# A decoder layer on one core: small operations on VectorE in the last ten steps, chunks of every sixteenth token, and a fixed order for the last chunk's projections

## The chip, the core and the metric

The kernel runs on one core of a Trainium2 chip. Five engines work side by side, each through a queue of its own in order: TensorE (PE in the profile; PEld is its weight load) multiplies matrices into PSUM, VectorE (DVE) and ScalarE (ACT) read PSUM and SBUF, GpSimd (POOL) works on SBUF alone here, and SyncE (SP) issues the DMAs. The metric is the device time of one execution in microseconds; the times of before are 2703.99, 2704.08 and 2704.45, median 2704.08.

## The reference

One pre-norm decoder layer over x of shape (2, 2048, 512) in float32, with three residual blocks. LN is a layer norm without scale and shift.

```
x = x + Wo . attention(rope(Wq . LN(x)), rope(Wk . LN(x)), Wv . LN(x))   # 16 heads of 32
x = x + gelu(LN(x) @ ctx.T) @ ctx                                        # 77 context rows
x = x + clip((LN(x) @ sign(W).T) * scale + bias, -100, 100)
```

The attention has no mask: each of the 2048 queries of a batch row looks at all 2048 keys. The rotary embedding turns each pair of features by an angle that depends on the token's place. All of the rest treats tokens alike.

## The kernel before

A *batch* is one of the two rows of x. Its 2048 tokens are cut into 16 *chunks* of 128 tokens, one token to a partition; four chunks make a *block* of 512. Chunk `ch` holds tokens `ch * 128` to `ch * 128 + 127`.

**Projections** (`project_batch`, L175). For each chunk: `norm` (L150 to L164) takes the mean and variance on VectorE (`chunk_stats`), makes scale and shift by four small operations (`scale_and_shift`, L141 to L146; the power by -0.5 in L143 always on GpSimd, from the constant tile `minus_half`), and applies them on ScalarE (L157). `turn` transposes the result on TensorE. `times` multiplies by `wk`, `wq` and `wv`; `rotate` applies the rotary tables `cos` and `sin` on VectorE and adds the halves on GpSimd (L212); `transpose_qk` turns q and k through TensorE into the tiles that attention reads (q copied by ScalarE, k by VectorE). The transposes of a chunk come one chunk late (`held`). In the loop TensorE is kept filled by `lead` (block maxima for the first attention steps) and by pieces of the output work of earlier blocks (`background_between`). The last chunk stands behind the loop, from L247: its projections, the transposes of two chunks, the values of the last two chunks, the last two sets of maxima, and the split and the transposition of the maxima of attention's first unit (`split_maxima`, `turn_maxima`).

Here the order is the tile scheduler's, which sorts the instructions by its own model of their times, with source order as priority.

**Attention** (`Attention.run`). A batch has 32 *units* (a block's 256 queries of four heads), each of eight *steps* over two chunks of keys at a time. A step has two halves of two heads each. In a half TensorE forms scores (L552, onto a start given by the maxima, L537), and in the same place the block maxima for the unit ten steps ahead (L459, reduced on VectorE, L471; `AHEAD = STEPS + 2` is 10). ScalarE takes the exponential (L690), GpSimd adds the two chunks' weights (`sm`, L692). A step later TensorE multiplies the weights by the values (L570), and another step later adds up the sums (`total`, L584). So in a batch's last ten steps there are no maxima and no reductions. In this part the order on TensorE, VectorE, ScalarE and GpSimd is the source's, by `tc.manual_schedule`; SyncE's is the scheduler's. The tiles `dkk`, `dkq` and `dkv` (differences between key blocks) lie in the buffers of `wk`, `wq` and `wv`, so the next batch's weights can be loaded only when these have been read for the last time.

**Output work** (`after_attention`). A generator for each finished part of a block: output projection, residual, norm, context attention, norm, feed-forward (L343 to L364), store. Its pieces are taken by `background`, one at a time, between the halves of attention's steps. Elementwise work that doesn't read PSUM goes where `side()` says:

```
    alone = []

    def side():
        return nc.vector if alone else nc.gpsimd
```

`alone` is set only behind the last batch's attention. Of batch 0's last block, the first two chunks are in the queue during the last ten steps; the other two are worked off in batch 1's projections. All parts of the last block of batch 1 go to the list `tail` and are worked off at the end, with `side()` on VectorE.

**Loads.** `load_x` brings a chunk to SBUF through SyncE, two chunks ahead; `cos` and `sin` are loaded once, each partition's 16 chunks in pieces of 64 bytes.

Of the kernel before, what the change touches and what calls it, by code (L numbers as in the profile page):

```python
# [9 lines left out]
F32 = mybir.dt.float32  # L10
F32R = mybir.dt.float32r
BF16 = mybir.dt.bfloat16
AF = mybir.ActivationFunctionType
# [3 lines left out]
P = 128  # L17
B, S, D = 2, 2048, 512
H, DK = 16, 32
C = 77  # L20
ND = D // P
BLK = 512
NB = S // BLK
CPB = BLK // P
NCH = S // P
HQ = 256
NU = NB * ND * 2
STEPS = NCH // 2
AHEAD = STEPS + 2
# [7 lines left out]
def decoder_layer(  # L37
# [16 lines left out]
    nc = tc.nc  # L54
# [11 lines left out]
    ps_acc = ctx.enter_context(tc.tile_pool(name="ps_acc", bufs=1, space=bass.MemoryType.PSUM))  # L66


    def load_x(b, ch, pool=xpool):
        t = pool.tile([P, D], F32, tag="x", name=f"x_{b}_{ch}")  # L70
        nc.sync.dma_start(t, x[b, ch * P : (ch + 1) * P, :])
        return t

    def load_w(src, name):
# [9 lines left out]
    qkv = load_qkv()  # L84
    cos = const.tile([P, NCH, DK // 2], F32, tag="cos", name="cos")
    sin = const.tile([P, NCH, DK // 2], F32, tag="sin", name="sin")
    nc.sync.dma_start(cos, rope_cos.rearrange("(c p) d -> p c d", p=P))
    nc.sync.dma_start(sin, rope_sin.rearrange("(c p) d -> p c d", p=P))

    ident = const.tile([P, P], F32, tag="ident", name="ident")  # L90
    make_identity(nc, ident)
# [4 lines left out]
    ones = const.tile([P, DK], F32, tag="ones", name="ones")  # L96
    nc.vector.memset(ones, 1.0)
    minus_half = const.tile([P, CPB], F32, tag="minus_half", name="minus_half")
    nc.vector.memset(minus_half, -0.5)


    mts = []
# [37 lines left out]
    def scale_and_shift(engine, stats):  # L140
        y, off = stats[:, :, 2], stats[:, :, 3]  # L141
        engine.tensor_scalar(y, stats[:, :, 1], EPS, None, ALU.add)
        nc.gpsimd.tensor_tensor(y, y, minus_half[:, : stats.shape[1]], ALU.pow)  # L143
        engine.tensor_mul(off, stats[:, :, 0], y)
        engine.tensor_scalar(off, off, -1.0, None, ALU.mult)
        return y, off  # L146

    def chunk_norm(ahead, b, ch):  # L150
        xc = ahead.pop(0)
        stats = stats_tile(1)
        chunk_stats(xc, stats[:, 0, 0:2])
        y, off = scale_and_shift(nc.gpsimd, stats)
        yield
        xn = work.tile([P, D], F32, tag="w", name="xn")
        nc.scalar.activation(xn, xc, AF.Identity, bias=off, scale=y)  # L157
        if ch + 2 < NCH:
            ahead.append(load_x(b, ch + 2))
        yield xn  # L160

    def norm(ahead, b, ch):
        *_, xn = chunk_norm(ahead, b, ch)
        return xn  # L164

    def turn(xn):
        pt = ps_t.tile([P, ND, P], F32, tag="t", name="pt")
        for i in range(ND):
            nc.tensor.transpose(pt[:, i, :], xn[:, i * P : (i + 1) * P], ident)  # L169
        xnt = work.tile([P, ND, P], F32, tag="w", name="xnt")  # L170
        nc.scalar.copy(xnt, pt)  # L171
        return xnt
# [3 lines left out]
    def project_batch(b, ahead, att, xnt, wk, wq, wv):  # L176
        def times(dst, xnt, w, part=range(ND)):
            for i in part:
                nc.tensor.matmul(dst, xnt[:, i, :], w[:, i, :], start=(i == 0), stop=(i == ND - 1))  # L179

        def transpose_qk(ch, qk, which=(0, 1)):
            blk, c = divmod(ch, CPB)
            cols = slice(c * P, (c + 1) * P)
            for a in which:
                pt = ps_s.tile([P, ND, P], F32, tag="s", name="ptqk")
                for i in range(ND):
                    nc.tensor.transpose(pt[:, i, :], qk[:, a, i * P : (i + 1) * P], ident)  # L187
                (nc.vector.tensor_copy if a else nc.scalar.copy)((att.q, att.k)[a][blk][:, :, cols], pt)
            if c == CPB - 1 and 1 in which:
                att.open_block(blk)  # L190

        def values(ch, xnt, pool=None):
            pv = (pool or ps_s).tile([P, D], F32, tag="t" if pool else "s", name="pv")
            times(pv, xnt, wv)
            v = kvq.tile([P, D], F32, tag=f"v{ch}", name=f"v_{b}_{ch}")
            nc.scalar.copy(v, pv)
            att.v.append(v)


        def rotate(ch, a, ps, r):  # L200
            half = [P, H, DK // 2]
            cs = cos[:, ch, None, :, None].to_broadcast(half + [2])
            sn = sin[:, ch, None, :].to_broadcast(half)
            pairs = ps.rearrange("p (h i t) -> p h i t", i=DK // 2, t=2)
            t1 = r[:, 0, a, :].rearrange("p (h i t) -> p h i t", i=DK // 2, t=2)
            t2 = r[:, 1, a, :].rearrange("p (h i t) -> p h i t", i=DK // 2, t=2)
            nc.vector.tensor_tensor(t1, pairs, cs, ALU.mult)
            nc.vector.scalar_tensor_tensor(
                t2[:, :, :, 0], pairs[:, :, :, 1], -1.0, sn, ALU.mult, ALU.mult
            )  # L210
            nc.vector.tensor_tensor(t2[:, :, :, 1], pairs[:, :, :, 0], sn, ALU.mult)  # L211
            nc.gpsimd.tensor_add(r[:, 0, a], r[:, 0, a], r[:, 1, a])  # L212

        held = None
        for ch in range(NCH):
            if ch == (NB - 1) * CPB:
                drain()
            blk, c = divmod(ch, CPB)
            if c == 0:
                att.q.append(kvq.tile([P, ND, BLK], F32, tag=f"q{blk}", name=f"q_{b}_{blk}"))  # L220
                att.k.append(kvq.tile([P, ND, BLK], F32, tag=f"k{blk}", name=f"k_{b}_{blk}"))
            r = big.tile([P, 2, 2, D], F32, tag="s", name="r")
            xn = norm(ahead, b, ch + 1) if ch + 1 < NCH else None
            pk = ps_t.tile([P, D], F32, tag="t", name="pk")
            pq = ps_t.tile([P, D], F32, tag="t", name="pq")
            if ch == NCH - 1:
                break
            times(pk, xnt, wk)
            rotate(ch, 1, pk, r)
            att.lead(1)  # L230
            background_between(2)
            times(pq, xnt, wq)
            rotate(ch, 0, pq, r)
            background_between(2)
            if held is not None:
                transpose_qk(*held)
            held = (ch, r[:, 0])
            xnt_next = turn(xn)
            if ch < NCH - 2:
                values(ch, xnt)  # L240
            else:
                left = xnt
            background_between(2)
            xnt = xnt_next


        times(pk, xnt, wk)  # L247
        rotate(ch, 1, pk, r)
        transpose_qk(*held)
        values(ch - 1, left, ps_t)  # L250
        transpose_qk(ch, r[:, 0], (1,))
        for i in range(ND):
            times(pq, xnt, wq, (i,))
            if i % 2 == 0:
                att.lead(1)
        rotate(ch, 0, pq, r)
        att.lead(AHEAD)
        values(ch, xnt, ps_t)
        transpose_qk(ch, r[:, 0], (0,))
        att.split_maxima(0)  # L260
        att.turn_maxima(0)
        att.key_steps()

    alone = []

    def side():
        return nc.vector if alone else nc.gpsimd


    attending = []
# [25 lines left out]
    def after_attention(b, blk, ot, first, end):  # L298
# [41 lines left out]
        def feed_forward(c, pt):  # L340
            parts = [work_tile([P, D], name, F32R) for name in ("high", "low")]
            parts = [part.rearrange("p (i t) -> p i t", t=P) for part in parts]
            nc.scalar.copy(parts[0], pt)  # L343
            nc.vector.tensor_sub(parts[1], pt, parts[0])
            yield True
            pf = bank([P, D], "pf")
            for k, part in enumerate(parts):
                for i in range(ND):
                    nc.tensor.matmul(  # L349
                        pf,  # L350
                        part[:, i, :],
                        wf[:, i, :],
                        start=(k == 0 and i == 0),
                        stop=(k == 1 and i == ND - 1),
                    )
            y = work_tile([P, D], "y")
            nc.vector.tensor_mul(y, pf, fs)
            yield False
            side().tensor_add(y, y, fb)
            yield False  # L360
            side().tensor_scalar(y, y, -MAX_VAL, MAX_VAL, ALU.max, ALU.min)
            side().tensor_add(xs[c], xs[c], y)
            r0 = blk * BLK + (first + c) * P
            nc.sync.dma_start(out[b, r0 : r0 + P, :], xs[c])  # L364
            yield False

        def project_out(ps, cols):
# [64 lines left out]
    class Attention:  # L432
# [201 lines left out]
        def run(self):  # L634
# [36 lines left out]
            more = self.b + 1 < B  # L671
            for t in range(NU * STEPS):
                u, i = divmod(t, STEPS)
                if more and t == (NU - 1) * STEPS:
                    self.x_next = [load_x(self.b + 1, 0), load_x(self.b + 1, 1)]
                if more and t == NU * STEPS - STEPS // 2:
# [38 lines left out]
            while ends:  # L715
                finish()
            attending.clear()
            ordered.__exit__(None, None, None)
            return xnt

    xnt = turn(norm(x_next, 0, 0))
    for b in range(B):
        att = Attention(b)
        project_batch(b, x_next, att, xnt, *qkv)
# [59 lines left out]
```

## Time and profile before

| | before |
|---|---|
| times of three runs | 2703.99, 2704.08, 2704.45 us |
| profiled execution | 2704.63 us, span 2702.9 us |
| mean granted clock of TensorE | 0.996 |
| busy: PE, DVE, ACT, POOL | 2675.5, 1702.1, 1321.0, 1741.2 us |
| batch 0: first projection, end of attention | 10.2, about 1339 us |
| batch 1: end of attention, last matmul ends | about 2655, 2696 us |

How to read it: the span runs from the first instruction to the last, and 1.7 us of the execution lie around it. Busy time is the union of an engine's instructions. In a list of waits a line has the waiting instruction, what released it, the microseconds in total, how often and the longest one. A line of the timeline has start, duration, engine, line of the kernel, operation, output and inputs, shapes, and in brackets the idle time of the engine ahead of it with what ended it. The granted clock is the share of full clock that TensorE had.

### The profile page before, as it was taken

The page shows a single profiled execution, that of the slowest core. Times are in us where ns is not written, and L with a number is a line of the kernel's source. Part 1 is how long each engine was busy: PE and PEld are TensorE (multiplying, and loading weights), DVE is VectorE, ACT ScalarE, POOL GpSimd, SP SyncE. Part 2 cuts the span into 40 slices and gives each one's busy share as a digit, 9 for nine tenths or more (in the row PEclk, how much of TensorE's full clock was granted, in tenths as well). Part 3 has the DMA queues.
Part 4 walks back from the last instruction along what each step waited for, and adds up shares of the span by engine and source line. Part 5 has one row for each costly group of instructions (what it writes and reads, how often), then busy time and mean ns, then how long its engine had stood idle before and what let it go on. Part 6 is the DMA issues. An engine that isn't in the chain of part 4 may idle for free.

```text
span 2702.9 us, 70221 instructions
## 1 busy us (share of the span) xinstructions
PE 2675.5 (99%) x30756; PEld 1490.6 (55%) x30756; DVE 1702.1 (63%) x2852; ACT 1321.0 (49%) x2393; POOL 1741.2 (64%) x1888
## 2 busy tenths in 40 slices
PE   8999999999999999999999999999999999999998
PEld 4445555555555555555554455555555555555555
DVE  3446777666666766676244467766767667766754
ACT  2114555455546554555422155555555455546553
POOL 3227777567857785677634287766687567857772
PEclk9999999999999999999999999999999999999999
DMA  4010000000000000000201000000000000000000
GB/s 125 24 32 2 5 4 4 4 4 18 20 3 4 11 28 4 4 12 26 72 25 36 8 4 4 4 4 4 4 27 12 4 4 19 19 4 4 19 19 17
DMA packets 41859, 43.54 MB, mean 16 GB/s; under 512 B 24758, under 2 KB 24758, under 8 KB 41552
## 3 DMA queue, kind: packets, MB, share of 16 engines
q1 hardware_dynamic: 41552, 39.05, 4.9%
q8 instruction: 241, 3.95, 0.6%
q14 instruction: 66, 0.54, 0.1%
HBM read 26.58 MB, written 8.39 MB: 13 GB/s over the span
## 4 chain that ended last, share of the span: by engine, by line
PE 96%; POOL 2%; DVE 1%; DMA 1%; issue 0%; ACT 0%; SPq 0%; POOLq 0%; ACTq 0%
PE st L552 22%; PE acc L570 22%; PE ps L459 18%; PE acc L584 8%; PE po L369 4%; PE pq L179 4%; PE pk L179 4%; PE pv L179 4%; PE st L537 3%; PE pf L349 2%; PE pt L331 1%; PE po L395 1%; PE ptqk L187 1%; PE ph L376 1%; POOL sm L692 1%; PE pt L169 1%
## 5 line engine op out<-in xcount | busy, mean ns | idle before, releaser
L692 POOL TENSOR_TENSOR sm<-pw 128x512 f32<-128x512 f32 x1024 | 1295.1, 1272 | 597.3 <-ACT pw L690 594.4
L471 DVE TENSOR_REDUCE mx<-ps 128x1 f32<-128x512 f32 x2048 | 1308.7, 682 | 515.6 <-PE ps L459 513.1
L690 ACT ACTIVATE pw<-st 128x512 f32<-128x512 f32 x2048 | 1111.4, 595 | 952.5 <-PE ps L459 618.4
L459 PE MATMUL ps<-k,q 32*128 32x512 f32 x4096 | 1188.3, 639 | 0.8 <-DVE mx L471 0.8
L570 PE MATMUL acc<-pw,v 128*32 128x256 f32 x8192 | 656.6, 392 | 0.0
L584 PE MATMUL acc<-sm,ones 128*32 128x128 f32 x7680 | 390.4, 280 | 2.1 <-POOL sm L692 2.1
L570 PEld LDWEIGHTS acc<-pw,v 128*32 128x32 f32 x8192 | 162.2, 108 | 398.1 <-issue 379.7
L459 PEld LDWEIGHTS ps<-k,q 32*128 32x128 f32 x4096 | 352.3, 183 | 21.5 <-issue 12.9
L584 PEld LDWEIGHTS acc<-sm,ones 128*32 128x32 f32 x7680 | 248.6, 110 | 157.3 <-POOL sm L692 2.6
L552 PE MATMUL st<-q,dkv 32*128 32x256 f32 x2048 | 291.8, 402 | 0.0
L552 PE MATMUL st<-q,dkk 32*128 32x256 f32 x2048 | 291.1, 400 | 0.0
L552 PE MATMUL st<-q,dkq 32*128 32x256 f32 x2048 | 289.9, 400 | 0.0
L552 PE MATMUL st<-q,k 32*128 32x256 f32 x2048 | 262.8, 374 | 0.0
L552 PEld LDWEIGHTS st<-q,dkk 32*128 32x128 f32 x2048 | 175.4, 184 | 89.8 <-issue 51.4
L552 PEld LDWEIGHTS st<-q,dkq 32*128 32x128 f32 x2048 | 172.7, 184 | 80.1 <-issue 54.2
L552 PEld LDWEIGHTS st<-q,dkv 32*128 32x128 f32 x2048 | 175.7, 185 | 59.5 <-issue 26.6
L552 PEld LDWEIGHTS st<-q,k 32*128 32x128 f32 x2048 | 195.0, 187 | 14.1
L212 POOL TENSOR_TENSOR r<-r 128x512 f32<-128x512 f32 x64 | 81.1, 1268 | 147.4 <-DVE r L211 147.0
L604 DVE RECIPROCAL num<-num 128x128 f32<-128x128 f32 x128 | 120.3, 942 | 63.1 <-ACT num L598 63.1
L133 DVE BATCH_NORM_STATS2 st<-x 128x6 f32<-128x512 f32 x96 | 65.4, 686 | 94.7 <-DMA x<-in_x_dram 94.4
L179 PE MATMUL pk<-wk,xnt 128*128 128x512 f32 x256 | 117.2, 601 | 2.3 <-ACT xnt L171 1.4
L179 PE MATMUL pq<-wq,xnt 128*128 128x512 f32 x256 | 118.0, 602 | 0.0
(106 smaller groups left out, 1788.2 us busy)
## 6 DMA issues: line engine op xcount, KB each, us to landing
x<-in_x_dram SPq DMA_DIRECT2D x64, 256.0 KB, 2.7
out_dram<-x SPq DMA_DIRECT2D x32, 256.0 KB, 2.0
wk<-in_wk_t_dram SPq DMA_DIRECT2D x2, 1024.0 KB, 8.4
wq<-in_wq_t_dram SPq DMA_DIRECT2D x2, 1024.0 KB, 10.7
wv<-in_wv_t_dram SPq DMA_DIRECT2D x2, 1024.0 KB, 6.1
wo<-in_wo_t_dram SPq DMA_DIRECT2D x1, 1024.0 KB, 6.3
wf<-in_wf_t_dram SPq DMA_DIRECT2D x1, 1024.0 KB, 5.1
mrow<-mt SPq DMA_TRANSPOSE x62, 2.3
```

The costliest lines, as they stand in the source:

```text
L179: nc.tensor.matmul(dst, xnt[:, i, :], w[:, i, :], start=(i == 0), stop=(i == ND - 1))
L212: nc.gpsimd.tensor_add(r[:, 0, a], r[:, 0, a], r[:, 1, a])
L369: nc.tensor.matmul(ps, ot[:, i, cols], wo[:, i, :], start=(i == 0), stop=(i == ND - 1))
L459: nc.tensor.matmul(ps, self.q[qb][self.rows[h], g, q0 : q0 + P], self.k[kb][self.rows[h], g, :], start=True, stop=True,)
L471: nc.vector.tensor_reduce(mx[:, qc, h, kb : kb + 1], ps, AX.X, ALU.max)
L537: nc.tensor.matmul(self.st[h], ones_b[r, :], mrow[r, None, :].to_broadcast([DK, 2, HQ]), start=True, stop=False, skip_group_check=True,)
L552: nc.tensor.matmul(self.st[h][:, c, :], keys[r, g, kc * P : (kc + 1) * P], self.q[qb][r, g, hf * HQ : (hf + 1) * HQ], start=False, stop=Tr ...
L570: nc.tensor.matmul(acc[self.rows[h], 0, :], self.v[self.chunk(i, c)][:, d0 : d0 + DK], pw[:, h, c, :], start=(i == 0 and c == 0), stop=(i ...
L584: nc.tensor.matmul(acc[self.rows[h], 1, part], ones, sm[:, h, part], start=False, stop=(i == STEPS - 1), skip_group_check=True,)
L604: nc.vector.reciprocal(num[:, 1, part], num[:, 1, part])
L690: nc.scalar.activation(pw[:, h], self.st[h], AF.Exp, scale=SCALE)
L692: nc.gpsimd.tensor_add(sm[:, hs, :], pw[:, hs, 0, :], pw[:, hs, 1, :])
```

## The change

It has five parts, all in one edit.

1. **Tokens.** Chunk `ch` holds every sixteenth token: partition p has token `16 p + ch`. `load_x` and the store use the new view `tokens`; `cos` and `sin` are laid out to match, so that a partition's 16 chunks are one run of 1 KB.
2. **Function table.** `minus_half` is written by a ScalarE activation (Identity, scale -0.5 on `ones`) and not by a VectorE memset, so the first activation, with the load of its function table, comes ahead of the first norm.
3. **First norm.** The small operations of the very first chunk's norm go to VectorE; the power stays on GpSimd.
4. **Last chunk.** The projections of the last chunk of each batch are put in source order on TensorE and VectorE. The order is new: the last chunk's queries are projected ahead of the values of the chunk before, the query rotation comes ahead of the maxima, and the two sets of maxima stand behind the first and the last quarter of those values. `values` is split, so that the copy (`keep_values`) stands by itself.
5. **Last ten steps.** From step `NU * STEPS - AHEAD` of a batch on, `free` is set, and `side()` gives VectorE to the output work's pieces until that batch's attention ends.

```diff
+    def tokens(rows, ch):
+        return rows.rearrange("(p c) d -> c p d", c=NCH)[ch]
...
-        nc.sync.dma_start(t, x[b, ch * P : (ch + 1) * P, :])
+        nc.sync.dma_start(t, tokens(x[b], ch))
...
-    nc.sync.dma_start(cos, rope_cos.rearrange("(c p) d -> p c d", p=P))
-    nc.sync.dma_start(sin, rope_sin.rearrange("(c p) d -> p c d", p=P))
+    nc.sync.dma_start(cos, rope_cos.rearrange("(p c) d -> p c d", p=P))
+    nc.sync.dma_start(sin, rope_sin.rearrange("(p c) d -> p c d", p=P))
...
-    nc.vector.memset(minus_half, -0.5)
+    nc.scalar.activation(minus_half, ones[:, :CPB], AF.Identity, scale=-0.5)
...
-    def chunk_norm(ahead, b, ch):
+    def chunk_norm(ahead, b, ch, engine=nc.gpsimd):
...
-        y, off = scale_and_shift(nc.gpsimd, stats)
+        y, off = scale_and_shift(engine, stats)
...
-    def norm(ahead, b, ch):
-        *_, xn = chunk_norm(ahead, b, ch)
+    def norm(ahead, b, ch, engine=nc.gpsimd):
+        *_, xn = chunk_norm(ahead, b, ch, engine)
...
             times(pv, xnt, wv)
+            keep_values(ch, pv)
+
+        def keep_values(ch, pv):
             v = kvq.tile([P, D], F32, tag=f"v{ch}", name=f"v_{b}_{ch}")
             nc.scalar.copy(v, pv)
             att.v.append(v)
...
+        ordered = tc.manual_schedule(
+            engines={mybir.EngineType.PE, mybir.EngineType.DVE}
+        )
+        ordered.__enter__()
         times(pk, xnt, wk)
         rotate(ch, 1, pk, r)
         transpose_qk(*held)
-        values(ch - 1, left, ps_t)
+        times(pq, xnt, wq)
         transpose_qk(ch, r[:, 0], (1,))
-        for i in range(ND):
-            times(pq, xnt, wq, (i,))
-            if i % 2 == 0:
-                att.lead(1)
         rotate(ch, 0, pq, r)
+        pv = ps_t.tile([P, D], F32, tag="t", name="pv")
+        times(pv, left, wv, (0,))
+        att.lead(1)
+        times(pv, left, wv, range(1, ND))
+        keep_values(ch - 1, pv)
         att.lead(AHEAD)
         values(ch, xnt, ps_t)
         transpose_qk(ch, r[:, 0], (0,))
         att.split_maxima(0)
         att.turn_maxima(0)
+        ordered.__exit__(None, None, None)
         att.key_steps()
...
     alone = []
+    free = []
 
     def side():
-        return nc.vector if alone else nc.gpsimd
+        return nc.vector if alone or free else nc.gpsimd
...
-            r0 = blk * BLK + (first + c) * P
-            nc.sync.dma_start(out[b, r0 : r0 + P, :], xs[c])
+            nc.sync.dma_start(tokens(out[b], blk * CPB + first + c), xs[c])
...
                 u, i = divmod(t, STEPS)
+                if t == NU * STEPS - AHEAD:
+                    free.append(True)
...
             attending.clear()
+            free.clear()
...
-    xnt = turn(norm(x_next, 0, 0))
+    xnt = turn(norm(x_next, 0, 0, nc.vector))
```

## The prediction

> **What bounds the kernel now.** The page first: TensorE is busy all through, so only its idle time and its clock can give anything.
>
> ```profile
> span 2702.9 us, 70221 instructions
> PE 2675.5 (99%) x30756; PEld 1490.6 (55%) x30756; DVE 1702.1 (63%) x2852; ACT 1321.0 (49%) x2393; POOL 1741.2 (64%) x1888
> ```
>
> Next the waits of TensorE: what it stood for, and the total. Together they are 20.7 us, and the tail behind its last matmul is 6.6 us more.
>
> ```profile
> PE pt L169 <- ACT xn L157: 8.1, 1, 8.1
> PE acc L584 <- POOL sm L692: 2.1, 1, 2.1
> PE pk L179 <- DMA wk<-in_wk_t_dram: 1.0, 1, 1.0
> PE ptqk L187 <- POOL r L212: 0.8, 1, 0.8
> PE ps L459 <- DVE mx L471: 0.8, 1, 0.8
> ```
>
> Then the timeline of TensorE around the 2.1 us wait, near the end of batch 0. Eight score matmuls (L552) take 1.13 us before it and 2.08 us behind it.
>
> ```profile
> 1320.10 1.13 PE L552 MATMUL st<-q,dkk 32*128 32x256 f32 x8
> 1325.99 0.41 PE L584 MATMUL acc<-sm,ones 128*32 128x128 f32 x4 [2.14 <-POOL sm L692]
> 1331.86 2.08 PE L552 MATMUL st<-q,dkv 32*128 32x256 f32 x8
> ```
>
> The windows view has busy time of PE, PEld, DVE, ACT and POOL (instructions in brackets), then the granted clock, DMA share and GB/s. The clock is halved in two stretches, each behind a wait: one behind the 0.76 us wait for `mx` in batch 0's last chunk, one behind the 2.14 us wait.
>
> ```profile
> 205.00:208.30 3.30, 2.54 (x10) 1.16 (x10) 3.28 (x6) 0.00 (x0) 0.00 (x0) 1.00 0.00 0
> 208.30:211.70 3.40, 3.40 (x5) 1.37 (x5) 3.05 (x7) 0.00 (x0) 1.64 (x3) 0.50 0.00 0
> 1320.10:1323.80 3.70, 3.70 (x48) 2.17 (x44) 0.00 (x0) 2.87 (x6) 3.62 (x4) 1.00 0.02 4
> 1328.00:1338.10 10.10, 10.10 (x88) 5.33 (x82) 0.00 (x0) 3.34 (x7) 5.37 (x5) 0.50 0.95 331
> ```
>
> The timeline of GpSimd says why `sm` was late: the feed-forward's L361 and L362 stand ahead of it in the queue, and five sums then run without a pause.
>
> ```profile
> 1320.19 1.27 POOL L692 TENSOR_TENSOR sm<-pw 128x512 f32<-128x512 f32 x1
> 1321.42 1.95 POOL L361 TENSOR_SCALAR y<-y 128x512 f32<-128x512 f32 x1
> 1323.45 1.26 POOL L362 TENSOR_TENSOR x<-x,y 128x512 f32<-128x512 f32 x1
> 1324.68 6.16 POOL L692 TENSOR_TENSOR sm<-pw 128x512 f32<-128x512 f32 x5
> ```
>
> Last, TensorE in the last chunk of batch 0 (first two lines) and batch 1. In batch 0 both maxima came together, and the second took 2.32 us where one takes 1.14, since banks came free one by one.
>
> ```profile
> 203.87 1.14 PE L459 MATMUL ps<-k,q 32*128 32x512 f32 x8
> 205.77 2.32 PE L459 MATMUL ps<-k,q 32*128 32x512 f32 x8 [0.76 <-DVE mx L471]
> 1548.03 1.21 PE L459 MATMUL ps<-k,q 32*128 32x512 f32 x8
> 1554.57 0.66 PE L187 MATMUL ptqk<-ident,r 128*128 128x128 f32 x4 [0.84 <-POOL r L212]
> ```
>
> **Last ten steps on VectorE.** They begin in batch 0 where the block maxima end, at 1286.6 us. From there GpSimd runs two each of L359 (1.28), L361 (1.93) and L362 (1.28), 9.0 us, and L142, L144 and L145 once for two chunks (0.66). These go to VectorE; the power (L143, 0.73) stays. There, by the rows of the kernel's end, an addition takes 0.69 and the clamp 0.42, so 2 x (0.69 + 0.42 + 0.69) = 3.6 us, and 3 x 0.15 for the small ones. VectorE was busy 7.8 of those 50 us. GpSimd keeps a 1.27 us sum per half step of 1.85 us; the late sum comes at least 4.5 us sooner (the second chunk's three operations) and was 2.1 us late. So the wait goes: 2.14 us. The half clock behind it lasted 10.24 us by the granted clock (1327.9 to 1338.1); at full rate that work takes half, so 5.12 us. Sum 7.26. Bounds: 2.14, if the clock drops anyway, to 7.26; I take the upper, as the clock is full all the way from 211.7 to the wait.
>
> The added wait is VectorE's, for the power, which stands behind a sum (1290.75 to 1292.02): it lasts from about 1288.5 to 1292.9. The next entry in VectorE's queue is L344, not due until 1297.3, so it holds nobody; ScalarE's `xn` at 1294.26 finds its operands some 0.5 us earlier than now. In batch 1 the same steps hold no such work (its last blocks go to the tail list, and GpSimd runs only sums and two L607 there): 0.
>
> What is late next at this place: weights. The SyncE queue issued batch 1's `wk` at 1327.13 behind the second store (1324.75, landed 1326.73) and an `x` load at 1326.75. The store now leaves at about 1317, so `wk` waits for the last read of `dkk`, which shares its buffer, at 1321.2. A 1 MB load alone took 6.1 us there (`wv`, 1334.00 to 1340.09), the slowest at the start 10.7. `wk` lands at 1327.3 to 1331.9; the first `pk` matmul is due at 1339.07 - 7.26 = 1331.8. `wq` (free at 1325.4, due 1335.3) and `wv` (1329.1, due 1342.6) have more room. I take 0, bound 0.1.
>
> **Last chunk in source order.** The same matmuls, transposes and copies, on two engines in a fixed order: `pk`, 8 transposes, `pq`, 4 transposes, a quarter of `pv`, maxima, the rest of `pv`, maxima, `pv` of the last chunk, 4 transposes, `ptm`. VectorE turns `q` before the eight reductions, no longer behind them, so GpSimd's addition of `r` is done some 5 us before its transposes: the 0.84 wait goes. The two maxima stand 3 quarters (2.6 us) apart, and four reductions (2.48 us) fit between, so banks are free: batch 0's 0.76, its long 2.32 and its half-clock stretch (3.41 us, worth 1.7) go. I size these by the two batches: from the first `pk` matmul to the first `st` matmul is 192.91 to 215.21 = 22.30 us in batch 0, 1535.72 to 1555.71 = 19.99 in batch 1. Without the 0.84, batch 1 needs 19.15. One new wait: the second maxima end at +14.2, four reductions 2.5, `neg` 0.2, five small GpSimd operations (0.26 to start, 1.4 to run) reach +18.4, where `ptm` could start at +18.1: 0.3 us. So 2.85 in batch 0 and 0.54 in batch 1, sum 3.39. The 0.38 wait for `mrow` stays. Batch 0 alone also has the sign conversions of `wf` (1.98 and 1.22 us, now at 198.59 and 202.00), which may fall between the reductions: 2.0 us lost there and 1.7 of half clock at worst, nothing at best; I take nothing, since VectorE has idle stretches of 2.7 and 1.2 us there. The part's ends are then -0.3 and +4.0.
>
> **The start.** The first norm on VectorE: at the kernel's end the chain from L142 to ScalarE takes 1.29 us (2660.44 to 2661.73), at the start 2.73 (4.53 to 7.26), so `xnt` is ready 1.4 us earlier, at about 8.4. But `wk` landed at 10.08 and the `pk` matmuls began at 10.22. Gain 0.1. The first table load (1.28 us) moves from 3.58 to about 1.1; it ended at 4.86 with its activation at 7.26, so 0; `minus_half` is then ready at about 2.6, before the power at 4.6. `cos` and `sin` become rows of 1 KB. Now they block SyncE (11.12 us of issue for `sin`) and with it the third `x` load until 15.27, yet TensorE has no wait from 10.22 to 192.2, so 0, whatever loads now pass them. Bounds: a late `wk` costs its lateness; at most 1.4 is to be had if `wk` landed with `xnt`, plus a clock that rises one 3.41 us window sooner (1.7).
>
> **Every sixteenth token.** An `x` load or store stays 128 rows of 2 KB, now 32 KB apart in memory. No row has this pitch. The nearest is the weight load: a partition's four 2 KB rows lie 256 KB apart, and 1 MB took 6.1 us, no slower per byte than `x` (256 KB in 2.7). The far one is `cos` in 64 B pieces, 12.9 us. I take 0. Only the first two loads and the last store are on the path; other loads run two chunks (23 us) ahead.
>
> **Sum.** 7.26 + 3.39 + 0.1 = 10.75. The profiled execution took 2704.63 (span 2702.9 and 1.7 around it), 0.55 over the median 2704.08; it gives 2693.9, and against the median 2693.3.
>
> **Rivals.**
> - *The clock does not follow the wait* (0.06). Half clock has another cause and stays; gains are 2.14 + 3.39 - 1.7 + 0.1 = 3.9: 2700.1. For it: waits of 0.68 and 0.84 elsewhere were followed by no drop. Against: the only half-clock stretches between 13.8 and 2683 us begin 2.5 and 1.9 us behind these two waits. The Trainium skill (TensorE: Matmul & The Clock Gate, What's actually happening) has the clock halve after a whole idle window of about 3.4 us, which neither wait is; by that rule this rival would hold, and the granted clock here speaks against it.
> - *The last chunk gives nothing* (0.14): the conversions fall between reductions, or GpSimd takes `dkv` (1.27 us) ahead of the split. Only 7.36: 2696.7.
> - *GpSimd stays late* (0.04): 3.5 remain, 2700.6.
> - *The wait moves to the weights* (0.07): an `x` load that waits for ScalarE's second norm (about 1333) gets ahead of `wk`; it lands at 1339.4, 7.6 us late, with 5.1 of half clock: 2693.3 + 12.7 = 2706.0, no measurable change.
> - *Slower: the pitch* (0.05). The `x` rows 32 KB apart crawl, and the first `wk` stands behind two such loads. It decides from 10.75 + 5.4 = 16.2 us, 8.1 per load: 256 KB in 10.9 us and not 2.8, and gives 2710. For it only the 12.9 us of `cos`, whose pieces are 64 B. The Trainium skill (DMA: Bandwidth & Descriptors, Latency and other measured facts) finds copies at half rate with rows 4 MiB apart and 207 GB/s at 512 KiB; it has no 32 KiB, and no run here shows such pitches. Half rate would cost this start about 2 us.
> - *`wk` comes early too* (0.04): 2690 to 2691.5.
>
> **How the numbers follow.** My forecast has 0.60, its own range 2691 to 2696. 0.2%, about what can be told from no change here, is 5.4 us: 2698.7 and 2709.5. Faster: 0.60 + 0.14 + 0.04 = 0.78; within: 0.06 + 0.04 + 0.07 = 0.17; slower 0.05. The range 2690.0 to 2700.5 holds the forecast, the last-chunk rival, the early `wk` and the unmoved clock, 0.84.
>
> **What would show it.** Right: no wait of `acc` for `sm`; granted clock 1.00 from 13.8 us to the tail; 19.4 us from `pk` to `st` in both batches; at most 0.3 before `ptm`; first `pk` near 10.1; `x` loads landing in 2.7. Wrong: half clock at either place without a wait ahead, a wait of batch 1's `pk` for `wk`, L114 or L116 among the last chunk's reductions, or `x` loads that take several us more.

## The result and the profile after

The changed kernel took 2692.95 us (median of six runs, 2692.05 to 2693.68) against 2704.23 for the kernel before beside it: a ratio of 0.9961, 95% interval 0.9951 to 0.9971. The forecast was 2693.3, faster. The profiled execution took 2693.15 us, its span 2691.0.

The page and then the waits of TensorE in the changed kernel (waiting instruction, what released it, us in total, times, longest):

```profile
span 2691.0 us, 70222 instructions
PE 2668.3 (99%) x30756; PEld 1490.3 (55%) x30756; DVE 1710.0 (64%) x2863; ACT 1321.0 (49%) x2394; POOL 1732.8 (64%) x1876
```

```profile
PE pt L173 <- ACT xn L161: 7.4, 1, 7.4
PE pt L345 <- ACT sparek L339: 4.9, 3, 4.1
PE pk L183 <- ACT xnt L175: 1.3, 2, 0.7
PE pk L183 <- DMA wk<-in_wk_t_dram: 1.0, 1, 1.0
PE st L550 <- DVE mrow L511: 0.8, 2, 0.4
```

The three waits that the change was to touch are gone from the list: `acc` for `sm` (2.1), `ptqk` for `r` (0.8) and `ps` for `mx` (0.8). Note the busy time of TensorE: 2668.3 and not 2675.5, with the same 30,756 matmuls. Seven of the twelve microseconds were never idle time. They were the same matmuls at half clock, and the windows view shows where they went (busy time of PE, PEld, DVE, ACT and POOL with instructions in brackets, then the granted clock, DMA share, GB/s):

```profile
205.00:208.30 3.30, 3.30 (x13) 1.27 (x12) 3.05 (x5) 0.58 (x1) 0.00 (x0) 1.00 0.00 0
208.30:211.70 3.40, 3.40 (x12) 1.64 (x10) 1.90 (x4) 0.17 (x1) 1.11 (x6) 1.00 0.00 0
1319.06:1322.80 3.74, 3.74 (x54) 2.25 (x50) 0.00 (x0) 2.91 (x6) 3.74 (x4) 1.00 0.71 261
1322.80:1328.90 6.10, 6.10 (x96) 3.70 (x92) 0.00 (x0) 3.12 (x6) 3.95 (x4) 1.00 0.89 292
```

The two places that had 0.50 have 1.00. Cut at the first matmul of each stage, the two profiled executions differ so:

| stretch | before | after | gained |
|---|---|---|---|
| start to the first `pk` | 10.22 | 9.55 | 0.67 |
| first `pk` to the last chunk's `pk`, batch 0 | 182.70 | 183.65 | -0.95 |
| last chunk, `pk` to `st`, batch 0 | 22.30 | 19.22 | 3.08 |
| `st` to batch 1's first `pk` | 1123.86 | 1116.49 | 7.37 |
| to the last chunk's `pk`, batch 1 | 196.65 | 196.78 | -0.13 |
| last chunk, batch 1 | 20.00 | 19.18 | 0.82 |
| attention of batch 1 | 1099.31 | 1098.78 | 0.53 |
| from the tail's first `po` to the end | 47.82 | 47.34 | 0.48 |

They sum to 11.87, the difference of the spans but for rounding.

In the last chunk of batch 0, TensorE now runs without a pause from `pk` to `ptm` (timeline: start, duration, instruction, shapes, count):

```profile
193.20 3.70 PE L183 MATMUL pk<-wk,xnt 128*128 128x512 f32 x8 [0.68 <-ACT xnt L175]
...
202.52 1.14 PE L472 MATMUL ps<-k,q 32*128 32x512 f32 x8
203.60 2.84 PE L183 MATMUL pv<-wv,xnt 128*128 128x512 f32 x6
206.37 1.49 PE L472 MATMUL ps<-k,q 32*128 32x512 f32 x8
...
212.42 0.39 PE L550 MATMUL st<-mrow,ones_b 32*128 32x512 bf16 x2 [0.38 <-DVE mrow L511]
```

The two maxima stand 3.85 us apart; the second takes 1.49 us where it took 2.32. On VectorE the query rotation (`r`) had stood behind the eight reductions. First the timeline of the kernel before, then that of the changed kernel, where it stands ahead of them:

```profile
205.02 4.88 DVE L471 TENSOR_REDUCE mx<-ps 128x1 f32<-128x512 f32 x8 [1.80 <-PE ps L459]
210.04 0.68 DVE L207 TENSOR_TENSOR r<-pq,cos 128x512 f32<-128x512 f32 x1
```

```profile
202.29 0.68 DVE L214 TENSOR_TENSOR r<-pq,cos 128x512 f32<-128x512 f32 x1
...
203.65 1.29 DVE L484 TENSOR_REDUCE mx<-ps 128x1 f32<-128x512 f32 x2
204.86 1.22 DVE L120 TENSOR_SCALAR signs<-wf 128x2048 fp32r<-128x2048 f32 x1
205.99 1.28 DVE L484 TENSOR_REDUCE mx<-ps 128x1 f32<-128x512 f32 x2
```

In the last ten steps, the five sums that GpSimd runs without a pause (its timeline):

```profile
1316.72 6.20 POOL L707 TENSOR_TENSOR sm<-pw 128x512 f32<-128x512 f32 x5
```

The second of them, counted from the batch's end, is the one that had come late. It runs from 1317.94 to 1319.22 and is done 1.5 us ahead of its reader (1320.69); before, it was done 2.1 us behind the time at which its reader was due.

### The profile page after: what moved, and what is told of

The parts are those of the page before. It is cut to its first block, busy times and chain, and to the rows that moved or that the text cites. A ratio compares the mean times of both kernels' runs of the same rounds, so it can differ in the third digit from the quotient of the medians.

```text
span 2691.0 us, 70222 instructions
## 1 busy us (share of the span) xinstructions
PE 2668.3 (99%) x30756; PEld 1490.3 (55%) x30756; DVE 1710.0 (64%) x2863; ACT 1321.0 (49%) x2394; POOL 1732.8 (64%) x1876
## 4 chain that ended last, share of the span: by engine, by line
PE 98%; DVE 1%; DMA 0%; issue 0%; ACT 0%; POOL 0%; SPq 0%; POOLq 0%; ACTq 0%
PE st L565 23%; PE acc L583 22%; PE ps L472 18%; PE acc L597 8%; PE po L382 4%; PE pk L183 4%; PE pq L183 4%; PE pv L183 4%; PE st L550 3%; PE pf L363 2%; PE pt L345 1%; PE po L408 1%; PE ptqk L191 1%; PE ph L389 1%; PE pt L173 1%; DMA wk<-in_wk_t_dram 0%
## 5 line engine op out<-in xcount | busy, mean ns | idle before, releaser
L382 PE MATMUL po<-wo,q 128*128 128x512 f32 x256 | 117.4, 603 | 0.0
```

The lines of the kernel that those rows point to most:

```text
L382: nc.tensor.matmul(ps, ot[:, i, cols], wo[:, i, :], start=(i == 0), stop=(i == ND - 1))
```

## The experiments

**The kernel before, once more.** No edit. One of its six times beside the change had been 2698.66 while five were near 2704.3, so its own spread was the first thing to explain.

> The kernel before once more, against itself, for the spread of its times: one of its six runs so far took 2698.7 us and five took 2704.0 to 2704.5. Theory: the 2.14 us wait of acc for sm is in every run, and what differs is how long the clock stays halved behind it. Then the times fall on levels about 5 us apart, 2698.7 and 2704.3, and the mean granted clock goes with them (0.998 and 0.996), since 5.1 us is half of 10.24. Rival: in the shorter run the wait itself was missing; then the levels lie 7 us apart or the clock does not go with the time.

Measured: 2704.1, with three of eleven runs at 2698.9 to 2699.1 and eight at 2703.2 to 2705.6. Of all 77 runs of the kernel before that served as the comparison, ten took 2698.7 to 2699.6, none lay between there and 2702.0, and 67 took 2702.0 to 2706.2. The profiled execution took 2705.14 and had the same wait and a longer half clock, in its windows:

```profile
1323.90:1326.90 3.00, 0.85 (x10) 0.57 (x10) 0.00 (x0) 0.46 (x1) 3.00 (x3) 1.00 0.23 87
1327.00:1340.50 13.50, 13.50 (x114) 7.01 (x110) 0.00 (x0) 3.84 (x7) 6.48 (x6) 0.50 0.79 273
205.00:208.30 3.30, 2.54 (x15) 1.02 (x16) 2.06 (x4) 0.00 (x0) 0.00 (x0) 1.00 0.00 0
208.30:211.70 3.40, 3.40 (x11) 1.43 (x11) 3.37 (x7) 0.00 (x0) 1.25 (x2) 1.00 0.00 0
```

Same program, same waits: at 1327 the half clock lasts 13.65 us here where it lasted 10.24, and at 208 it is not there at all. So a wait's price in clock is not fixed. No execution near 2699 was profiled here; the run of the order alone, below, shows a wait without half clock.

**The last ten steps alone.** The kernel before with `free` and nothing else:

```diff
+    free = []
...
-        return nc.vector if alone else nc.gpsimd
+        return nc.vector if alone or free else nc.gpsimd
...
+                if t == NU * STEPS - AHEAD:
+                    free.append(True)
...
+            free.clear()
```

> Only the last ten steps' small operations go to VectorE; all else is the kernel before. Theory: the wait of acc for sm goes and with it the 10.24 us of half clock, 7.3 us in all: 2696.9 us, the last chunk as before (22.3 us from pk to st in batch 0, 20.0 in batch 1). Rival, the clock does not follow the wait: half clock stays near 1328 us, 2.1 us gained, 2702.1.

Measured: 2696.33 (2695.89 to 2696.89) against 2704.52, ratio 0.9968 (0.9957 to 0.9980). The wait of `acc` is gone, `st` to the next `pk` takes 1116.49 us as in the full change, and no run lies on a second level: all six are within 1.0 us. The gain is 8.2 us and not 7.3. That stretch is 7.37 us shorter than in the first profile of before, with 10.24 us of half clock, and 8.91 shorter than in the repeat, with 13.65; the median of before is taken over both kinds and the runs near 2699.

**The last chunk's order alone.** The kernel before with the new sequence inside `tc.manual_schedule` and nothing else.

> Only the last chunk's new sequence in source order; all else is the kernel before. Theory: 19.2 us from pk to st in both batches, 3.1 and 0.8 us gained, half clock at 208 us gone; the 2.1 us wait of acc for sm and its half clock stay: 2700.3 us. Rival, the gains of the two places are not independent (an earlier start of attention moves the later wait): anything from 2697 to 2704, and the wait of acc is no longer 2.1 us.

Measured: 2699.77, ratio 0.9982 (0.9973 to 0.9991), in two groups: four of eleven runs took 2695.8 to 2696.7, seven 2699.4 to 2701.9. The last chunk took 19.22 and 19.19 us. The profiled execution fell in the lower group, and shows the wait with full clock behind it, as I take it to be in the kernel before at 2699 too. Timeline of TensorE:

```profile
1319.73 1.13 PE L561 MATMUL st<-q,dkq 32*128 32x256 f32 x8
1323.79 0.41 PE L593 MATMUL acc<-sm,ones 128*32 128x128 f32 x4 [2.15 <-POOL sm L701]
1324.14 1.13 PE L561 MATMUL st<-q,dkq 32*128 32x256 f32 x8
1325.99 1.13 PE L561 MATMUL st<-q,dkv 32*128 32x256 f32 x8
```

Eight score matmuls take 1.13 us ahead of the wait and behind it. So the same wait of 2.14 to 2.16 us cost itself alone in this profile, and in others itself and 5.1 us (10.24 us at half clock) or 6.8 us (13.65). The two runs near 2699.5 lie 3.5 us above the lower group, which neither figure gives; no such execution was profiled.

The starts and ends of all half-clock stretches of one profile lie on a grid of 3.41 us (here the first rise at 15.45 and an end at 2681.26 are 781 steps apart), and the grid lies elsewhere in each execution. Counting from 15.45, a step ends at 1322.76: it cuts this wait, which runs from 1321.64 to 1323.79, into 1.12 and 1.03 us. In the profile of before the cut is at 1324.48, into 0.63 and 1.51, and the clock drops at the end of that second step, at 1327.89. In the repeat the whole 2.15 us lie in one step. At this place the clock dropped in the six profiles in which 1.46 us or more of the wait fell in one step (before, its repeat, and further down the old sequence, the tokens, the start and the fourteen additions). It dropped in neither of the two in which at most 1.12 us did (this one, and the seven additions, where the wait is cut into 0.71 and 0.45). That is no threshold for other places: at 208 us the clock dropped in two profiles behind a step with 0.76 us of idle time, and in the tail of the last run below behind one with 0.83 (see what stays open). The Trainium skill (TensorE: Matmul & The Clock Gate, What's actually happening) has such a free-running window of about 3.4 us, and the grid here agrees with it; its condition of a whole idle window does not hold here, where 1.46 us of one were enough.

**A wait put back, short and long.** The changed kernel, with idle additions on GpSimd ahead of the late sum (the tile `idle` is made and zeroed at the start, not shown here):

```diff
+                    if more and heads[0] == 0 and t == NU * STEPS - 4:
+                        for _ in range(7):
+                            nc.gpsimd.tensor_add(idle, idle, idle)
```

The second run has `range(14)`.

> The changed kernel with seven GpSimd additions of 128x96 on a tile of its own (about 2.6 us in all) ahead of the first sum that runs late there, in batch 0's fourth step from the end; they compute nothing that is used. In the changed kernel that sum is done about 1.4 us ahead of its reader, so a wait of acc for sm of about 1.2 us comes back. Theory, the clock follows a wait of more than about a microsecond within one 3.4 us stretch: 1.2 us and 1.7 to 5.1 us of lost clock, 2695.9 to 2699.3. Rival, a wait this short leaves the clock alone (0.84 us did): 2694.2.

> The same with fourteen such additions (about 5.2 us): a wait of about 3.8 us. Theory: half clock of one to three stretches of 3.4 us behind it, 3.8 + 1.7 to 5.1: 2698.5 to 2701.9. Rival, the clock does not follow the wait: 2696.8 and granted clock 1.00 at this place.

Measured: 2694.14 with seven (four runs, 2693.81 to 2694.43) and 2703.32 with fourteen (ten runs, 2701.61 to 2704.47). With seven, first from the waits of TensorE, then the windows:

```profile
PE acc L599 <- POOL sm L709: 1.2, 1, 1.2
```

```profile
1320.00:1322.00 2.00, 0.84 (x12) 0.49 (x10) 0.00 (x0) 0.53 (x2) 2.00 (x3) 1.00 1.01 366
1322.00:1329.00 7.00, 7.00 (x107) 4.26 (x107) 0.00 (x0) 3.85 (x7) 6.65 (x6) 1.00 0.68 237
```

With fourteen, the same two views:

```profile
PE acc L599 <- POOL sm L709: 4.1, 1, 4.1
```

```profile
1320.60:1325.00 4.40, 0.27 (x6) 0.14 (x4) 0.00 (x0) 0.43 (x1) 3.93 (x9) 1.00 0.61 231
1325.00:1338.60 13.60, 13.60 (x104) 7.24 (x104) 0.00 (x0) 3.84 (x7) 7.18 (x6) 0.50 0.46 154
```

A wait of 1.16 us costs 1.2 us, and one of 4.13 costs 10.4 (2703.32 - 2692.95): itself, 6.8 for 13.65 us at half clock, less 0.6. The clock follows the longer wait. For the first I had expected a drop as well, and the rival that so short a wait leaves the clock alone came true (2694.2); for the second I had put the lost clock at 5.1 us at most, and it was more. The additions put the sums off by 2.86 and 5.83 us, so these have 1.7 us of slack in the changed kernel, where I had read 1.4.

**Source order with the old sequence.** The kernel before, its old last chunk put inside `tc.manual_schedule` for TensorE and VectorE.

> The last chunk in source order on TensorE and VectorE, but in the old sequence (values of the chunk before, then the queries in quarters with the maxima between, the query rotation last); all else is the kernel before. Theory, both the fixed order and the new sequence count: the two maxima of batch 0 stand apart again, so batch 0 falls to batch 1's 20.0 us and its half clock at 208 us goes, 2.3 us gained: 2701.9; the 0.8 us wait of ptqk for r stays in both batches. Rival, the new sequence does it all: 2704.2. Rival, the fixed order does it all: 19.2 us in both batches, 2700.3.

Measured: 2704.03 against 2704.52, ratio 1.0000 (0.9991 to 1.0009). A fixed order with the old sequence gains nothing that these runs can tell: the last chunk takes 20.58 and 20.59 us, better than 22.30 in batch 0 (21.29 where the half clock is missing) and worse than 20.00 in batch 1. The timelines of VectorE and then TensorE in batch 0 of this run:

```profile
206.74 2.48 DVE L476 TENSOR_REDUCE mx<-ps 128x1 f32<-128x512 f32 x4 [0.53 <-PE ps L464]
209.14 0.68 DVE L207 TENSOR_TENSOR r<-pq,cos 128x512 f32<-128x512 f32 x1
210.40 0.18 DVE L483 TENSOR_REDUCE neg<-mx 128x8 f32<-128x32 f32 x1
```

```profile
211.88 0.66 PE L187 MATMUL ptqk<-ident,r 128*128 128x128 f32 x4 [0.60 <-POOL r L212]
213.19 0.28 PE L500 MATMUL ptm<-ident_b,mt 128*128 128x128 bf16 x2 [0.65 <-POOL mt L489]
```

The maxima stand apart now, but the query rotation waits behind the eight reductions and holds up `neg` as well, so each batch has two waits of 0.60 to 0.66 us, where the profile of before has one (0.76 in batch 0, 0.84 in batch 1). The scheduler had placed `neg` ahead of the rotation by itself. What gains is the new sequence: with the rotation ahead of the reductions, neither wait is in its trace. Its other moves were not tried one by one.

**Tokens alone, and the start alone.** First the `tokens` view with the tables' layout; then `minus_half` on ScalarE with the first norm on VectorE; each on the kernel before.

> Only the chunks of every sixteenth token, with the cos and sin tables in rows of 1 KB; all else is the kernel before. Theory: hidden; x loads land in 2.7 us as before, SyncE is no longer blocked for 11 us by sin, TensorE has no wait from the first pk to the last chunk either way: 2704.2 us, within 1.5 us (the place of the first clock rise). Rival, rows 32 KB apart are slow: the first x lands later than 3.5 us, and wk behind it; 2706 or more. Rival, the freed SyncE queue is worth something: 2702 or less.

> Only the first norm on VectorE and the function table first; all else is the kernel before. Theory: xnt is ready 1.4 us earlier, wk lands at about 10 as before and holds the first pk: 0.1 us, 2704.1. Rival: the first pk goes with xnt, 1 us or more earlier and the clock rises earlier too: 2701 to 2703.

Measured: 2704.03 for the tokens, ratio 0.9996 (0.9987 to 1.0006), and 2704.87 for the start, 1.0002 (0.9993 to 1.0011). Neither is to be told from nothing. With the tokens alone, SyncE's queue is free at 6 us and not at 15 (its timeline):

```profile
4.42 1.60 SPq L92 DMA_DIRECT2D sin<-in_rope_sin_dram  x1
8.24 2.83 SPq L75 DMA_DIRECT2D x<-in_x_dram  x2
```

The issue of `sin` takes 1.60 us where it took 11.12, and TensorE's last chunk begins at 192.83 us as it did at 192.91. With the start alone, the first transposes come at 7.19 and not 8.12, the first `pk` at 9.76 and not 10.22, and the last chunk at 193.35: nothing is left of it in this profile, where the clock rose at 15.10 and not 13.76.

**Only the clamp on VectorE.** The changed kernel, with the feed-forward's two additions back on GpSimd in the last ten steps:

```diff
-            side().tensor_add(y, y, fb)
+            (nc.vector if alone else nc.gpsimd).tensor_add(y, y, fb)
...
-            side().tensor_add(xs[c], xs[c], y)
+            (nc.vector if alone else nc.gpsimd).tensor_add(xs[c], xs[c], y)
```

> The changed kernel, but in the last ten steps the two additions of each chunk (L373 and L376) go back to GpSimd; the clamp and the small norm operations stay on VectorE. GpSimd so gets 2 x 2 x 1.28 = 5.1 us back. Theory: the sums have about 1.4 us to spare in the changed kernel, the second chunk's two additions (2.6 us) take it and leave a wait of acc for sm of about 1.2 us; like the 1.16 us wait with seven additions it leaves the clock alone: 2694.2 us. Rival, moving the clamp is enough: no wait, 2693.0. Rival, a wait of 2 us and half clock as in the kernel before: 2699 to 2702.

Measured: 2692.87, ratio 0.9962 (0.9948 to 0.9976), no wait of `acc`. My expectation of 2694.2 missed: moving the clamp, the costliest of the three on GpSimd (1.93 us each), with the small norm operations is enough. I had added the two additions to the sums' delay as if nothing else moved. In the trace VectorE's statistics for the next batch's first norm end at 1311.5, no longer held up by the second clamp (1313.5 in the changed kernel), and that norm's operations on GpSimd begin at 1311.58 and not 1313.25, ahead of a sum (1312.71) and no longer behind one (1311.89).

**Beyond the change.** In the changed kernel a wait of 0.68 us stays ahead of the last `pk` of each batch, and one of 1.0 for `wk` at the start. In the last turn of the loop, the input's transposes ahead of those of q and k:

```diff
-            if held is not None:
-                transpose_qk(*held)
+            if ch == NCH - 2:
+                xnt_next = turn(xn)
+            transpose_qk(*held) if held is not None else None
             held = (ch, r[:, 0])
-            xnt_next = turn(xn)
+            if ch < NCH - 2:
+                xnt_next = turn(xn)
```

> The changed kernel, and in the last turn of the projection loop the transposes of the last chunk's input (pt) come ahead of the eight transposes of q and k, so that ScalarE's copy of xnt runs beside these. Theory: the two waits of 0.68 us of the last pk for xnt go, 1.4 us: 2691.6. Rival, the wait turns into one for a copy of q or k later in the last chunk: 2693.0.

Measured: 2690.96 (five runs, 2690.70 to 2691.28), ratio 0.9955 (0.9942 to 0.9968). Both waits are gone. The 2.0 us gained are more than their 1.4; where the rest is from was not looked for. Then, on top of it, `wk` ahead of the second x chunk:

```diff
-    x_next = [load_x(0, 0), load_x(0, 1)]
-    qkv = load_qkv()
+    x_next = [load_x(0, 0)]
+    qkv = [load_w(wk_t, "wk")]
+    x_next.append(load_x(0, 1))
+    qkv += [load_w(w, name) for w, name in ((wq_t, "wq"), (wv_t, "wv"))]
```

> The same, and at the start wk is loaded ahead of the second x chunk. Theory: wk lands some 0.7 us earlier (256 KB at the 350 GB/s of that stretch) and the first pk goes with it; the clock rises when the 3.4 us grid says, so the median gains 0.3 to 0.7 on the run before this one: 2691.1. Rival, wk's landing is set by one slow DMA engine and not by what is queued ahead: 2691.6.

Measured: 2692.74, worse by 1.8 than without. `wk` did land early, at 6.95 us, but the queue of VectorE shows what took its place:

```profile
4.41 0.15 DVE L148 TENSOR_SCALAR stats<-stats 128x1 f32<-128x1 f32 x1
7.61 0.69 DVE L139 BATCH_NORM_STATS2 st<-x 128x6 f32<-128x512 f32 x1 [3.04 <-DMA x<-in_x_dram]
8.54 0.15 DVE L150 TENSOR_TENSOR stats<-stats 128x1 f32<-128x1 f32 x1
```

The second chunk's statistics wait for its x, and the first norm's last two operations (L150, L151) stand behind them; TensorE's first transposes fall back from 7.14 to 9.84. With `wq` too ahead of the second x, the scheduler puts the first norm first:

> The run turn_first, and at the start the order of loads is first x chunk, wk, wq, second x chunk, wv. In turn_and_wk wk landed at 6.95 instead of 9.77, but VectorE's queue held the first norm's last two operations behind the statistics of the second chunk, whose x landed at 7.58, and TensorE's first transposes fell back to 9.84. Here the first norm stands ahead of these statistics in VectorE's queue. Theory: the first transposes at about 6.4, the first pk at about 8.4 and not 9.9; the clock's rise still goes by its grid, so about 1 us in the median: 2689.9. Rival: the second chunk, now late, is missed at its own transposes near 19 us: 2691 or more. Rival: the earlier pk falls into half clock and gains less than 0.5: 2690.6.

VectorE's queue of this run, with the same two operations now 0.9 us apart and not 4.1:

```profile
4.62 0.15 DVE L148 TENSOR_SCALAR stats<-stats 128x1 f32<-128x1 f32 x1
...
5.51 0.16 DVE L150 TENSOR_TENSOR stats<-stats 128x1 f32<-128x1 f32 x1 [0.60 <-POOL stats L149]
```

Measured: 2689.90 (2689.45 to 2691.59), ratio 0.9946 (0.9932 to 0.9959). The first `pk` is at 8.61 and waits only for `xnt`. This is the lowest median of all, 3 us below the change; its five runs overlap with those of the run before the loads were moved (2690.70 to 2691.28).

## Why the prediction was right, step by step

- **The sum.** 2693.3 forecast, 2692.95 measured; 10.75 us of gain forecast against the profiled execution, 11.86 between the two spans. Part of the nearness is luck, as the next points show.
- **Last ten steps, 7.26.** Right in mechanism: `sm` is in time, the wait is gone, the half clock with it; 7.37 in the profiles, 8.2 alone. The late sum came 3.6 us sooner by its reader's time (from 2.1 late to 1.5 early), where I had said at least 4.5; it was enough. The term was sized on one draw. The wait's price in clock was 0, 5.1 or 6.8 us: whether it is paid went with where the grid cuts the wait, and what sets its size is open. I took 5.12 as a fixed price because one profile showed it; without half clock the stretch took 1119.05 us in the run with the order alone, 2.56 above the 1116.49 of the change, so there this part is worth 2.6, of which the wait explains 2.15.
- **The added wait of VectorE for the power.** Forecast 4.4 us, held by nobody. Measured 4.21, and no TensorE wait behind it. What I did not see is in the last section.
- **The weights at the join.** Forecast: `wk` waits for the last read of `dkk`, no longer for the second store. It was issued at 1318.41, just behind that read (1318.3) and the x load at 1316.24, and `pk` at 1328.92 did not wait.
- **Last chunk, 2.85 + 0.54.** Measured 3.08 + 0.82. The 0.3 us wait of `ptm` was none in batch 0 and 0.14 in batch 1. Again the size of batch 0 was that of one draw: 22.30 held 3.41 us of half clock, which the repeat of before did not have (21.29). So the half clock there was worth 1.0 and not the 1.7 that I put on it: without it, a wait of 0.47 us of `ptqk` for `r` came back. The conversion L120 (L116 before) did fall among the first four reductions (204.86), which I had named as a sign of being wrong and priced at 2.0 us and 1.7 of half clock at worst; it held up the second maxima by 0.35 us (1.49 and not 1.14) and no more.
- **The start, 0.1.** `pk` came 0.67 sooner, as `wk` landed at 9.42 and not 10.08, and the clock rose at 15.02 and not 13.76, so the last chunk began 0.28 later. The sum took the clock's first rise as fixed, and that step failed: it came between 13.1 and 17.2 us over the profiles here. In two executions of the kernel before it came at 13.76 and 16.21, and the stretch from the first `pk` to the last chunk's was 1.22 us longer in the second (183.92), more than the edit is worth.
- **Every sixteenth token, 0.** Confirmed: 0.9996, and the first x landed 2.7 to 3.1 us behind its issue in the kernels with rows 32 KB apart, and 2.8 in the kernel before.
- **The rivals.** That the clock does not follow the wait is refuted by the fourteen additions (4.13 us cost 10.4) and the reverse, that it always follows, by the seven and by the order alone. None of the others occurred; of the second, that the last chunk gives nothing, one conversion fell between reductions, at the price above.

What stays open: why the half clock lasts three steps in one execution and four in another; 0.4 us of the 2.56 above; and how much idle time drops the clock elsewhere. At 208 us, where matmuls are held up one by one (2.54 us busy in 3.30), it dropped in two of the five profiles with the scheduler's order, and the same 0.76 us wait lay whole in one step in all five. In the tail of the last run above it dropped at 2666.34, behind a step with waits of 0.50 and 0.33 us; the rest of the second wait, 3.8 us, lies behind the drop. The two parts alone gain 8.2 and 4.8 us by their medians, 1.7 more than together (11.3); the order alone had four of eleven runs without half clock where the kernel before had ten of 77, and I can't tell that from chance.

## What to carry to other kernels

Look at the granted clock behind a wait before pricing it: on the busiest engine a wait of about two microseconds cost here two to nine, and moving queued work off the engine that is late paid back the clock as well as the wait. Repeat the profile of before when its times lie on levels, since a term read from one execution can be one of several draws. Fixing an order pays only if the sequence is the right one: what others wait for goes ahead of the bulk work on its engine.

## What the runs showed that I had not expected

**VectorE and GpSimd hold each other up.** The moved operations took longer than at the kernel's end, where GpSimd runs no sums. Timelines of VectorE and GpSimd in the changed kernel:

```profile
1289.85 1.24 DVE L148 TENSOR_TENSOR stats<-stats 128x2 f32<-128x2 f32 x1 [4.21 <-POOL stats L147]
1301.08 1.03 DVE L375 TENSOR_SCALAR y<-y 128x512 f32<-128x512 f32 x1
1302.15 1.74 DVE L376 TENSOR_TENSOR x<-x,y 128x512 f32<-128x512 f32 x1
```

```profile
1289.79 1.28 POOL L707 TENSOR_TENSOR sm<-pw 128x512 f32<-128x512 f32 x1
1302.06 1.27 POOL L707 TENSOR_TENSOR sm<-pw 128x512 f32<-128x512 f32 x1 [0.23 <-ACT pw L705]
1303.30 0.90 POOL L620 TENSOR_TENSOR q<-num 128x128 f32<-128x128 f32 x1
```

A multiplication of two columns (L148) takes 1.24 us, where one column takes 0.16 at the kernel's end: it starts 0.06 us behind a sum on GpSimd and ends 0.02 us behind the sum's end. The clamp takes 1.03 and not 0.42, the addition L376 1.74 and not 0.69, and GpSimd's L620, which started while L376 ran, 0.90 and not 0.45. The subtraction L358, which reads one of its inputs from PSUM, ran beside sums at its usual 0.69 us (1294.37 and 1306.38). The Trainium skill (SBUF — State Buffer, Who interferes with whom) states that a VectorE instruction with two SBUF inputs and a GpSimd instruction that reads SBUF exclude each other, the later one waiting to the end; the trace agrees for L148, L376 and L620, with these numbers. The clamp, with one input, was slowed as well, which that sentence does not cover. It cost TensorE nothing here, as VectorE had room, but 3.6 us of moved work became 5.9 (0.63 + 1.03 + 1.74 + 0.69 + 1.16 + 0.69), and L620, 0.45 us longer, took back part of GpSimd's relief.

**The order of the loads moved small operations on another engine.** Loading `wk` ahead of the second x chunk made the kernel 1.8 us slower, and moving that chunk behind `wq` too made it 2.8 us faster again. In the traces, the place of the second chunk's statistics in VectorE's queue, which the scheduler chooses, went with the order of the loads: ahead of the first norm's last two operations in the one, behind them in the other.
